# Six of eight layer norms turned by VectorE blocks and a trip through DRAM instead of by TensorE

## The chip, the core and the metric

The kernel runs on one core of a Trainium2 chip. The metric is the time of one execution on the device, in microseconds (us). The engines are named as the profile names them: PE is TensorE (PEld its weight loads), DVE is VectorE, ACT is ScalarE, POOL is GpSimd and SP is SyncE, whose queue issues most of the DMAs. Each engine works through its own list of instructions in order; an instruction that has to wait holds up all that stand behind it on the same engine.

## The reference: what is computed

For four sequences (b = 0 to 3) of 512 rows of 512 numbers, in float32, one block of a transformer with cross-attention:

```python
h1 = layer_norm(x, ln1_w, ln1_b)                    # over the 512 numbers of a row
q = h1 @ q_w + q_b;  k = enc @ k_w + k_b;  v = enc @ v_w + v_b   # 16 heads of 32
a = softmax(mask(q k^T / sqrt(32))) v
hidden = a @ cproj_w + cproj_b + x
y = layer_norm(hidden, ln2_w, ln2_b)
out = hidden + gelu(y @ fc_w + fc_b) @ proj_w + proj_b   # fc: 512 -> 2048, proj: 2048 -> 512
```

There are thus two layer norms per sequence, eight in all. They are called (1,b) and (2,b) here.

## The kernel before, in words

**What a turn is.** A matrix product on PE sums over the partitions, so the normalised rows (`xn`, rows on the partitions) have to be turned: features onto the partitions, rows along them. The four tiles of a norm (128 rows by 512 features, `t` = 0 to 3) become one tile of four feature groups (`d` = 0 to 3), each 128 by 512. For the first norms the target is `xT`, the second half of the tile `xe`; for the second norms it is `yT`. `ln_turn` (lines 150 to 161) does it for one `d`: four PE transposes into a PSUM tile `tp` (L156), then one eviction that also applies the norm's weight and bias, which after the turn belong to partitions: by DVE (L159) for d = 1 and 2, or by ACT (L161). For the norms in `BY_ACT`, (1,1) and (1,2), ACT does all four.

**The attention loop.** 16 head groups (`w` = 4b + g, four heads each) with four quarters of queries (`qt`) make 64 stages. A stage, called (w,qt), computes four score tiles on PE into the one PSUM tile `sc` (`scores`, L259); DVE adds the mask and finds the row minimum (L263, four times, called "minima"); ACT takes the exponential with its sum (L267, four times); DVE transposes the result in blocks of 32 by 32 (`turn`, L282 and L290) into `tb`. There are six slots for score tiles, and `sc` is single, so the next scores wait for the minima of the stage before. After two stages SP copies `tb` into `pT` with 16 DMAs, which swap the 32-partition blocks (L325), and some stages later PE multiplies with v (`attend`, L342) and DVE normalises (L347).

**What is laid between the stages.** For each head group `prep_k`, `prep_q`, `prep_v` (acck L215, accq L225, accv L237, some 3.5 us of PE each, evicted by ACT; POOL then adds the bias of v, L249). `prep_q` reads `xT`, so it needs the turned first norm of its sequence. After the four groups of a sequence comes `cproj` (accc L383, four chains), whose sum is `hidden`, then the second norm; then the chains `fc` (accf L449, reads `yT`) and `proj` (accp L459), taken a few at a time by `some(n)`. The order is written out by hand: `first[w]` is a list of work for head group w. A tuple gives one list for each of its four stages, run right after the stage's scores and block transposes were issued; a plain list is spread over the stages by cost, and `later[w]` is added to it from the third stage. `inputs(b)` returns the loads of x, the three parts of the first norm, its turn, and the load of enc.

**The end.** From about 558 us `last_mlps` computes the remaining MLP (half of sequence 1, and all of 2 and 3) by a scheme with seven products of blocks. `fc_pair` (L553) makes the hidden layer; `project` (L593) multiplies with proj in the order q1, q2, q3, q6, q7, q5, q4. Between q1 and q2 `sums` loads the next sequence's hidden rows, to which POOL adds a bias (L354); between q2 and q3 `turns` turns the second norm of the next sequence; POOL and DVE add the products to the hidden rows (`join`, L531), SP stores them; `middle` then makes the sums of blocks of `yT` (`y_sums`, DVE L481) and of the first weights (`sum_wa`, DVE L481 and L484), which the next `fc_pair` reads.

The statistics of a norm are DVE's (L125, L126), the reciprocal root is POOL's (L131, L133), and the normalisation DVE's (L147) or, for `BY_ACT`, ACT's (L143).

Of the kernel before, what the change touches and what calls it, by code (L numbers as in the profile page):

```python
# [12 lines left out]
F32 = mybir.dt.float32  # L13
U8 = mybir.dt.uint8
AF = mybir.ActivationFunctionType
# [5 lines left out]
P = 128  # L21
B, L, D, H = 4, 512, 512, 16
HD = D // H
INNER = 4 * D
NT = L // P
ND = D // P
# [5 lines left out]
NI = P // HD  # L32
# [15 lines left out]
LN1W, LN1B, QB, KB, LN2W, LN2B, FCB = 0, 4, 8, 12, 16, 20, 24  # L48
# [4 lines left out]
def xattn_block(ctx: ExitStack, tc: tile.TileContext, x, encT, mask, q_w, k_w, v_w, c_w, fc_w, p_w, vecs, rows, out):  # L53
    nc = tc.nc
    scale = float(np.float32(1.0) / np.sqrt(HD).astype(np.float32))

    def pools(stack, **bufs):
        return [stack.enter_context(tc.tile_pool(name=n, bufs=k)) for n, k in bufs.items()]

    const, keep, hids, tiles, small = pools(ctx, const=1, keep=1, hids=6, tiles=4, small=4)  # L60
    dram = ctx.enter_context(tc.tile_pool(name="dram", bufs=1, space=bass.MemoryType.DRAM))
    ps_acc = ctx.enter_context(tc.tile_pool(name="ps_acc", bufs=4, space=PSUM))

# [6 lines left out]
    vec = const.tile([P, NVEC], F32, tag="vec", name="vec")  # L70
# [9 lines left out]
    eT, xT = (xe[:, i * ND * L : (i + 1) * ND * L].rearrange("p (d l) -> p d l", d=ND) for i in range(2))  # L80
# [9 lines left out]
    def k_q(w, i):  # L90
        n = w % 4 * 2 + i
        return pbt[:, n * D : (n + 1) * D]
# [16 lines left out]
    def kqv_w(w, i):  # L109
        n = 4 * i + 2 + w % 2  # L110
        return ptt[:, n * D : (n + 1) * D].rearrange("p (d f) -> p d f", d=ND)

    S = {}
    count = [0, 0, 0]
# [12 lines left out]

    def ln_rs(key):

        ve = small.tile([P, NT], F32, tag="ve", name=f"ve{key[0]}_{key[1]}")  # L130
        nc.gpsimd.tensor_scalar(ve, S["mv", key][:, :, 1], EPS, 1.0, ALU.add, ALU.mult)  # L131
        rs = small.tile([P, NT], F32, tag="rs", name=f"rs{key[0]}_{key[1]}")
        nc.gpsimd.tensor_tensor(rs, ve, nhalf, ALU.pow)  # L133
        S["rs", key] = rs
        if key in BY_ACT:
            nm = small.tile([P, NT], F32, tag="nm", name=f"nm{key[0]}_{key[1]}")
            nc.gpsimd.tensor_tensor(nm, S["mv", key][:, :, 0], rs, ALU.mult)
            nc.gpsimd.tensor_scalar(nm, nm, -1.0, 0.0, ALU.mult, ALU.add)
            S["nm", key] = nm

    def ln_norm(key, t, dst, src):
        if key in BY_ACT:
            nc.scalar.activation(  # L143
                dst, src, AF.Identity, bias=S["nm", key][:, t : t + 1], scale=S["rs", key][:, t : t + 1]
            )
            return
        nc.vector.tensor_scalar(  # L147
            dst, src, S["mv", key][:, t, 0:1], S["rs", key][:, t : t + 1], ALU.subtract, ALU.mult
        )

    def ln_turn(key, d, xn, dst):

        w, bi = (LN1W, LN1B) if key[0] == 1 else (LN2W, LN2B)
        tp = acc_tile(f"tp{key[0]}_{key[1]}_{d}")
        for t in range(NT):
            nc.tensor.transpose(tp[:, ts(t, P)], xn[t][:, ts(d, P)], ident)  # L156
        wd, bd = vec[:, w + d : w + d + 1], vec[:, bi + d : bi + d + 1]
        if d in (1, 2) and key not in BY_ACT:
            nc.vector.tensor_scalar(dst[:, d, :], tp, wd, bd, ALU.mult, ALU.add)  # L159
        else:  # L160
            nc.scalar.activation(dst[:, d, :], tp, AF.Identity, bias=bd, scale=wd)  # L161


    def queue(b):
        return Q[0] if b else nc.sync

    def load_enc(b):
        for d in range(ND):
            queue(b).dma_start(out=eT[:, d, :], in_=encT[b, ts(d, P), :])

    def load_x(b):
        S["xn", b] = [tiles.tile([P, D], F32, tag="xn", name=f"xn1_{b}_{t}") for t in range(NT)]
        for t in range(NT):
            queue(b).dma_start(out=S["xn", b][t], in_=x[b, ts(t, P), :])

# [11 lines left out]
    def ln1_turn(b, d):  # L187
        ln_turn((1, b), d, S["xn", b], xT)
# [167 lines left out]
    def stays(b, t):  # L356

        return b == 0 or b == SPLIT and t < 2

    def load_h(b, *ts_):  # L360

        if ("xa", b) not in S:
            S["xa", b] = dram.tile([L, D], F32, tag=f"xa{b}", name=f"xa{b}")
        for t in ts_:
            if b == B - 1:

                S["h", b, t] = k_q(t // 2, t % 2)
            else:
                pool, tag = (hids, "hid") if stays(b, t) else (tiles, "xn")
                S["h", b, t] = pool.tile([P, D], F32, tag=tag, name=f"h_{b}_{t}")  # L370
# [17 lines left out]
    def load_xn(b):  # L388

        for t in range(NT):  # L390
            S["h", b, t] = tiles.tile([P, D], F32, tag="xn", name=f"hn_{b}_{t}")
            Q[0].dma_start(out=S["h", b, t], in_=S["xa", b][ts(t, P), :])

    def load_hid(b, ts_):
# [10 lines left out]

    def norm2(b, t):
        h = S["h", b, t]
        y = tiles.tile([P, D], F32, tag="xn", name=f"xn2_{b}_{t}") if stays(b, t) else h
        S.setdefault(("yn", b), {})[t] = y
        ln_norm((2, b), t, y, h)  # L410

    def proj_bias(b):
        for t in range(NT):
            if stays(b, t):
                add_row(S["hid", b, t], 1)

    def ln2_turn(b, d):
        if d == 0:
            S["yT", b] = keep.tile([P, ND, L], F32, tag="yT", name=f"yT_{b}")
        ln_turn((2, b), d, S["yn", b], S["yT", b])  # L420


    weights, products = [], []
# [281 lines left out]

    def C(b):
        return [(CHAIN, lambda t=t: cproj(b, t)) for t in range(NT)]

    def turns1(b):
        return [(TURN, lambda d=d: ln1_turn(b, d)) for d in range(ND)]  # L710

    def turns2(b):
        return [(TURN, lambda d=d: ln2_turn(b, d)) for d in range(ND)]

    def FC(b, q):
        return [(CHAIN, lambda f=f: fc(b, f)) for f in range(q * FQ, (q + 1) * FQ)]
# [3 lines left out]

    def inputs(b):
        ln = [(0.0, lambda part=part: ln1(b, part)) for part in range(3)]
        return do(lambda: load_x(b)), ln, turns1(b), do(lambda: load_enc(b))

    def run(work, budget=None):

# [33 lines left out]
    x1, x2, x3, x4 = inputs(1)  # L760
# [9 lines left out]
    first = [[] for _ in range(NW)]  # L770
    later = [[] for _ in range(NW)]
# [17 lines left out]
    def some(n):  # L789
        taken, mlp[:n] = mlp[:n], []  # L790
        return taken
# [24 lines left out]
    k, q, v = A(7)  # L816
    c, t2 = C(0), turns2(0)
    first[4] = x1 + [k, q, v] + x4
    later[4] = c[:1] + x2[:1] + c[1:2] + x2[1:2] + c[2:3] + x2[2:] + c[3:]
    k, q, v = A(8)  # L820
    first[5] = (
        [k] + stat(0, 0, 1, 2, 3) + rs(0) + x3 + norm(0, 0, 1, 2, 3) + [v], [q] + t2, some(2) + pb_(0), some(2)
    )
    k, q, v = A(9)
    x1, x2, x3, x4 = inputs(3)
    first[6] = [k, q] + some(4) + [v] + x1
    k, q, v = A(10)
    first[7] = [k, q] + x2[:1] + some(2) + x2[1:2] + some(3) + [v]

    k, q, v = A(11)  # L830
    first[8] = h_(1, 0, 1) + x2[2:] + [k, q] + x3[:2] + some(1) + x3[2:3] + [v] + x3[3:] + h_(1, 2, 3) + x4
    later[8] = cb(1) + C(1)
    k, q, v = A(12)
    first[9] = [q] + some(2) + [k] + some(2) + [v]
    k, q, v = A(13)
    first[10] = [k, q] + some(4) + [v]
    k, q, v = A(14)
    t2 = turns2(1)
    first[11] = (
        [k, q] + stat(1, 0, 1, 2, 3) + rs(1), some(2) + norm(1, 0, 1, 2, 3), some(1) + t2[:2] + [v],  # L840
        t2[2:] + pb_(1) + some(1) + h_(2, 2, 3, 0, 1)
    )

    k, q, v = A(15)
    c = C(2)
# [49 lines left out]
    c = C(B - 1)  # L895
# [49 lines left out]
```

## Time and profile before

| what | value |
|---|---|
| time, median of 3 runs | 810.9 us (808.69 to 811.1) |
| the profiled execution: time / span of its instructions | 810.09 us / 808.3 us |
| mean granted TensorE clock | 0.996 |
| busy: PE | 791.9 us (98% of the span) |
| busy: DVE, ACT, POOL | 553.6, 360.8, 98.0 us |
| PE transposes of the turns (L156) | 128, 18.7 us busy in all |
| DMA | 137.13 MB, mean 170 GB/s |
| POOL's own DMA queue (q0) | 2.82 MB |

The span runs from the first to the last instruction; the time of the execution is 1.79 us longer. A time such as "at 168 us" counts from the start of the span. Idle time of an engine is put down to what released it. A matmul's row gives the time from its start to its modelled end; the step from one row's start to the next is the time it takes from PE.

### The profile page before, as it was taken

How to read it: one execution, taken by the hardware profiler on the slowest of the kernel's cores; microseconds unless marked ns; L12 is line 12 of the kernel's file. 1: busy time of each engine (PE TensorE's matmuls, PEld its weight loads, DVE VectorE, ACT ScalarE, POOL GpSimd, SP SyncE). 2: the span in 40 equal slices, each digit the busy share in tenths (PEclk: the TensorE clock that was granted, in tenths of full speed). 3: DMA queues.
4: the chain of work that ended last, by engine and by line, in shares of the span. 5: the costliest groups of instructions: out<-in, count | busy, mean ns of one | idle time of the engine just before them, and what ended most of it. 6: DMA issues, size and time to landing. Idle time of an engine off the chain costs nothing.

```text
span 808.3 us, 11790 instructions
## 1 busy us (share of the span) xinstructions
PE 791.9 (98%) x4082; PEld 481.2 (60%) x4082; DVE 553.6 (68%) x1145; ACT 360.8 (45%) x785; POOL 98.0 (12%) x112
## 2 busy tenths in 40 slices
PE   9999999979999999999999999999999999999998
PEld 6545455544454544535554333446888888888887
DVE  3788998876678665877778997636738993368511
ACT  2666755638673646556643469600312330023200
POOL 1110030030000030001131000120050021200011
PEclk9999999989999999999999999999999999999999
DMA  9889989837797877778768799883335330023001
GB/s 329 287 222 244 241 219 265 225 96 185 185 245 176 223 201 191 176 197 201 177 140 218 196 259 226 216 252 117 108 100 181 107 117 14 27 79 92 1 14 39
DMA packets 60955, 137.13 MB, mean 170 GB/s; under 512 B 12464, under 2 KB 15664, under 8 KB 60768
## 3 DMA queue, kind: packets, MB, share of 16 engines
q1 hardware_dynamic: 59472, 132.43, 61.2%
q0 software_dynamic: 896, 2.82, 1.1%
q10 hardware_dynamic: 528, 1.14, 0.7%
q8 instruction: 32, 0.52, 0.3%
q14 instruction: 27, 0.22, 0.1%
HBM read 58.22 MB, written 6.82 MB: 80 GB/s over the span
## 4 chain that ended last, share of the span: by engine, by line
PE 80%; DVE 7%; SPq 7%; DMA 3%; issue 1%; POOL 0%; ACT 0%; DVEq 0%; POOLq 0%
PE q L553 15%; PE accf L449 9%; PE accp L459 8%; PE accc L383 7%; SPq L325 7%; PE av L342 6%; PE sc L259 6%; PE acck L215 4%; PE accq L225 4%; PE accv L237 4%; DVE ptt L263 3%; PE q5p L593 2%; PE q3p L593 2%; PE q7p L593 2%; PE q6p L593 2%; PE q1p L593 2%
## 5 line engine op out<-in xcount | busy, mean ns | idle before, releaser
L267 ACT ACTIVATE ptt<-ptt,mn 128x512 f32<-128x512 f32 x256 | 182.2, 713 | 142.8 <-DVE mn L263 142.6
L263 DVE CUSTOM_DVE_ANT_0 ptt<-sc,mb 128x512 f32<-128x512 f32 x256 | 161.1, 685 | 45.6 <-PE sc L259 45.5
L282 DVE STREAM_TRANSPOSE tb<-ptt 128x1024 f32<-128x1024 f32 x96 | 119.1, 1242 | 10.4 <-ACT ptt L267 8.0
L449 PE MATMUL accf<-yT,pbt 128*128 128x512 f32 x192 | 87.3, 601 | 0.0
L459 PE MATMUL accp<-pbt,gt 128*128 128x512 f32 x192 | 86.5, 600 | 0.0
L259 PE MATMUL sc<-pbt 32*128 32x512 f32 x512 | 73.1, 640 | 4.8 <-DVE mn L263 2.6
L553 PE MATMUL q<-ys,gt 128*128 128x256 f32 x320 | 75.1, 379 | 0.0
L553 PEld LDWEIGHTS q<-ys,gt 128*128 128x128 f32 x320 | 60.8, 190 | 8.3
L449 PEld LDWEIGHTS accf<-yT,pbt 128*128 128x128 f32 x192 | 35.0, 190 | 50.2 <-issue 45.4
L459 PEld LDWEIGHTS accp<-pbt,gt 128*128 128x128 f32 x192 | 35.2, 190 | 48.8 <-issue 45.8
L237 PEld LDWEIGHTS accv<-ptt,xe 128*128 128x128 f32 x512 | 58.9, 192 | 8.2 <-issue 5.4
L237 PE MATMUL accv<-ptt,xe 128*128 128x128 f32 x512 | 60.5, 276 | 0.0
L215 PE MATMUL acck<-xe,ptt 128*128 128x512 f32 x128 | 59.0, 603 | 0.0
L553 PE MATMUL q<-yT,gt 128*128 128x256 f32 x240 | 58.1, 379 | 0.5 <-DVE gt L481 0.5
L225 PE MATMUL accq<-xe,ptt 128*128 128x512 f32 x128 | 58.4, 599 | 0.0
L383 PE MATMUL accc<-wc,oT 128*128 128x512 f32 x128 | 56.6, 596 | 0.0
L249 POOL TENSOR_TENSOR v<-v,row 128x512 f32<-128x512 f32 x16 | 20.4, 1274 | 278.5 <-ACT v L242 278.4
L557 ACT ACTIVATE ga<-uc,vec 128x256 f32<-128x256 f32 x40 | 20.4, 511 | 75.5 <-DVE uc L531 75.5
L553 PEld LDWEIGHTS q<-yT,gt 128*128 128x128 f32 x240 | 45.5, 190 | 7.4 <-DVE gt L481 0.9
L342 PE MATMUL av<-pT,v 128*32 128x256 f32 x768 | 48.1, 392 | 1.6 <-DMA pT<-tb 1.5
L267 ACT ACTIVATION_READ_ACCUMULATOR ptt<-ptt,mn 128x1 f32 x256 | 48.3, 189 | 0.0
L564 ACT COPY p<-q 128x256 f32<-128x256 f32 x20 | 7.1, 354 | 92.0 <-PE q L553 92.0
(121 smaller groups left out, 957.9 us busy)
## 6 DMA issues: line engine op xcount, KB each, us to landing
pT<-tb SPq DMA_DIRECT2D x384, 136.0 KB, 2.4
pbt<-p_w_dram SPq DMA_DIRECT2D x40, 256.0 KB, 3.1
gt<-fc_w_dram SPq DMA_DIRECT2D x40, 256.0 KB, 2.7
gt<-tb SPq DMA_DIRECT2D x64, 136.0 KB, 3.4
xe<-tb SPq DMA_DIRECT2D x56, 136.0 KB, 3.3
pbt<-fc_w_dram SPq DMA_DIRECT2D x24, 256.0 KB, 4.3
ptt<-k_w_dram SPq DMA_DIRECT2D x16, 256.0 KB, 3.9
xe<-encT_dram SPq DMA_DIRECT2D x16, 256.0 KB, 4.8
```

The costliest lines, as they stand in the source:

```text
L215: nc.tensor.matmul(acc, S["wk", w][:, d, :], eT[:, d, :], start=(d == 0), stop=(d == ND - 1))
L225: nc.tensor.matmul(acc, S["wq", w][:, d, :], xT[:, d, :], start=(d == 0), stop=(d == ND - 1))
L237: nc.tensor.matmul(acc[:, ts(t, P)], eT[:, d, ts(t, P)], S["wv", w][:, d, :], start=(d == 0), stop=(d == ND - 1),)
L259: nc.tensor.matmul(sc[:, h, :], qT[r, ts(qt, P)], kT[r, :], start=True, stop=True)
L263: nc.vector.tensor_tensor_reduce(out=s, in0=sc[:, h, :], in1=S["mb", w // NG], scale=1.0, scalar=FMAX, op0=ALU.add, op1=ALU.min, accum_out=mn,
L267: nc.scalar.activation(s, s, AF.Exp, bias=mn, scale=-1.0, accum_out=sums[:, qt, h : h + 1])
L282: nc.vector.transpose(*two_heads[k])
L342: nc.tensor.matmul(av[ts(h, HD), : 2 * P].rearrange(shape, **kw), v[:, t, ts(h, HD)], p[t][h], start=(t == 0), stop=(t == NT - 1),)
L383: nc.tensor.matmul(acc, S["oT", b][:, g, ts(t, P)], wc[:, g, :], start=(g == 0), stop=(g == NG - 1))
L449: nc.tensor.matmul(acc, S["fcw", b, f][:, d, :], S["yT", b][:, d, :], start=(d == 0), stop=(d == ND - 1))
L459: nc.tensor.matmul(acc, gT[q % 2][:, k, ts(t, P)], S["pw", b, q * FQ + k], start=(k == 0), stop=(k == FQ - 1))
L553: nc.tensor.matmul(o, a[:, k], y[:, k], start=(k == 0), stop=(k == 1))
```

## The change: what it does

Norms (1,0) and (1,1) are turned as before. The other six, (1,2), (1,3) and (2,0) to (2,3), are turned in three steps:

- `ln_flip`: DVE transposes 32 by 32 blocks of each of the four tiles (four instructions of 128x512), into the target tile itself, in an order that puts each block row together;
- `ln_swap`: POOL's queue writes that tile to DRAM (one DMA of 128 rows of 8 KB, 1 MB) and, when it has landed, reads it back into a new tile `raw` with four DMAs of 32 partitions (256 KB each), so that the 32-partition blocks change places;
- `ln_affine`: ACT applies weight and bias from `raw` to the target, four instructions of 128x512.

The pool `tiles` with its four slots becomes the one tile `xnt` with four parts, used in turn; `raw` takes 8 KB of each partition, and the area for the descriptors of POOL's DMAs is set to 8192. The order of the work around the turns changes: in `first[4]` to `first[11]` the steps have places of their own.

```diff
+    xnt = const.tile([P, NT * D], F32, tag="xnt", name="xnt")
+    raw = const.tile([P, NT * D], F32, tag="raw", name="raw")
...
+    def ln_flip(key, xn, dst):
+
+        tmp = dst.rearrange("p d l -> p (d l)").rearrange("p (j c t q) -> p t c j q", j=NI, c=ND, t=NT)
+        for t in range(NT):
+            nc.vector.transpose(tmp[:, t], xn[t])
+
+    def ln_swap(key, dst):
+
+        turned = dram.tile([NI, HD, NI, D], F32, tag="turned", name=f"turned{key[0]}_{key[1]}")
+        nc.gpsimd.dma_start(out=turned.rearrange("i a j n -> (i a) (j n)"), in_=dst.rearrange("p d l -> p (d l)"))
+        for j in range(NI):
+            nc.gpsimd.dma_start(
+                out=raw[ts(j, HD), :].rearrange("p (i n) -> p i n", i=NI), in_=turned[:, :, j, :].rearrange("i a n -> a i n")
+            )
+
+    def ln_affine(key, dst):
+
+        w, bi = (LN1W, LN1B) if key[0] == 1 else (LN2W, LN2B)
+        rv = raw.rearrange("p (i c t q) -> p c t i q", i=NI, c=ND, t=NT)
+        for d in range(ND):
+            nc.scalar.activation(
+                dst[:, d, :].rearrange("p (t i q) -> p t i q", t=NT, i=NI), rv[:, d], AF.Identity,
+                bias=vec[:, bi + d : bi + d + 1], scale=vec[:, w + d : w + d + 1],
+            )
...
-    def ln2_turn(b, d):
-        if d == 0:
+    def ln2_turn(b, step):
+        if step == 0:
             S["yT", b] = keep.tile([P, ND, L], F32, tag="yT", name=f"yT_{b}")
-        ln_turn((2, b), d, S["yn", b], S["yT", b])
+            ln_flip((2, b), S["yn", b], S["yT", b])
+        elif step == 1:
+            ln_swap((2, b), S["yT", b])
+        else:
+            ln_affine((2, b), S["yT", b])
...
     first[4] = x1 + [k, q, v] + x4
-    later[4] = c[:1] + x2[:1] + c[1:2] + x2[1:2] + c[2:3] + x2[2:] + c[3:]
-    k, q, v = A(8)
+    later[4] = c[:1] + x2[:1] + c[1:2] + x2[1:2] + c[2:3] + x2[2:]
     first[5] = (
-        [k] + stat(0, 0, 1, 2, 3) + rs(0) + x3 + norm(0, 0, 1, 2, 3) + [v], [q] + t2, some(2) + pb_(0), some(2)
+        x3[:1] + c[3:] + stat(0, 0, 1, 2) + [k8] + x3[1:2], stat(0, 3) + rs(0) + norm(0, 0, 1, 2, 3) + [v8] + x3[2:],
+        t2[:1] + [q8, v9] + t2[1:2], [k9, q9] + t2[2:] + pb_(0)
     )
...
-    first[6] = [k, q] + some(4) + [v] + x1
+    first[6] = some(7) + x1
...
-    first[8] = h_(1, 0, 1) + x2[2:] + [k, q] + x3[:2] + some(1) + x3[2:3] + [v] + x3[3:] + h_(1, 2, 3) + x4
-    later[8] = cb(1) + C(1)
+    first[8] = h_(1, 0, 1) + x2[2:] + [k, q] + x3[:1] + some(1) + x3[1:2] + [v] + h_(1, 2, 3) + x4
+    later[8] = cb(1) + C(1) + x3[2:]
...
-    first[9] = [q] + some(2) + [k] + some(2) + [v]
+    first[9] = [q] + some(3) + [k] + some(2) + [v]
...
-        [k, q] + stat(1, 0, 1, 2, 3) + rs(1), some(2) + norm(1, 0, 1, 2, 3), some(1) + t2[:2] + [v],
+        [k, q] + stat(1, 0, 1, 2, 3) + rs(1), some(2) + norm(1, 0, 1, 2, 3), t2[:1] + some(1) + [v] + t2[1:2],
         t2[2:] + pb_(1) + some(1) + h_(2, 2, 3, 0, 1)
...
-    nc = bacc.Bacc("TRN2", target_bir_lowering=False, num_devices=1)
+    nc = bacc.Bacc("TRN2", target_bir_lowering=False, num_devices=1, dynamic_dma_scratch_size=8192)
```

Here `x3` and `t2` are now the three steps flip, swap and affine of a first and of a second norm, `c` the four chains of `cproj`, and `k8`, `q8`, `v8` the preparations of head group 8. In `last_mlps`, `turns` still calls the three steps of the next sequence's second norm between q2 and q3.

More of the change, by code (lines that the diff above doesn't have):

```diff
@@ L58, in pools @@
         return [stack.enter_context(tc.tile_pool(name=n, bufs=k)) for n, k in bufs.items()]
-    const, keep, hids, tiles, small = pools(ctx, const=1, keep=1, hids=6, tiles=4, small=4)
+    const, keep, hids, small = pools(ctx, const=1, keep=1, hids=6, small=4)
     dram = ctx.enter_context(tc.tile_pool(name="dram", bufs=1, space=bass.MemoryType.DRAM))
@@ L111, in kqv_w, with xn_tile @@
         return ptt[:, n * D : (n + 1) * D].rearrange("p (d f) -> p d f", d=ND)
+    xnt = const.tile([P, NT * D], F32, tag="xnt", name="xnt")
+    raw = const.tile([P, NT * D], F32, tag="raw", name="raw")
+    def xn_tile():
+        n = count[3] % NT
+        count[3] += 1
+        return xnt[:, n * D : (n + 1) * D]
     S = {}
-    count = [0, 0, 0]
+    count = [0, 0, 0, 0]
     Q = [nc.sync]
@@ L171, in load_x @@
     def load_x(b):
-        S["xn", b] = [tiles.tile([P, D], F32, tag="xn", name=f"xn1_{b}_{t}") for t in range(NT)]
+        S["xn", b] = [xn_tile() for t in range(NT)]
         for t in range(NT):
@@ L368, in load_h @@
             else:
-                pool, tag = (hids, "hid") if stays(b, t) else (tiles, "xn")
-                S["h", b, t] = pool.tile([P, D], F32, tag=tag, name=f"h_{b}_{t}")
+                S["h", b, t] = hids.tile([P, D], F32, tag="hid", name=f"h_{b}_{t}") if stays(b, t) else xn_tile()
             Q[0].dma_start(out=S["h", b, t], in_=x[b, ts(t, P), :])
@@ L390, in load_xn @@
         for t in range(NT):
-            S["h", b, t] = tiles.tile([P, D], F32, tag="xn", name=f"hn_{b}_{t}")
+            S["h", b, t] = xn_tile()
             Q[0].dma_start(out=S["h", b, t], in_=S["xa", b][ts(t, P), :])
@@ L407, in norm2 @@
         h = S["h", b, t]
-        y = tiles.tile([P, D], F32, tag="xn", name=f"xn2_{b}_{t}") if stays(b, t) else h
+        y = xn_tile() if stays(b, t) else h
         S.setdefault(("yn", b), {})[t] = y
@@ L710, in turns1, with flips1 @@
         return [(TURN, lambda d=d: ln1_turn(b, d)) for d in range(ND)]
+    def flips1(b):
+        return [
+            (0.0, lambda: ln_flip((1, b), S["xn", b], xT)),
+            (0.0, lambda: ln_swap((1, b), xT)),
+            (0.0, lambda: ln_affine((1, b), xT)),
+        ]
     def turns2(b):
-        return [(TURN, lambda d=d: ln2_turn(b, d)) for d in range(ND)]
+        return [(0.0, lambda n=n: ln2_turn(b, n)) for n in range(3)]
     def FC(b, q):
@@ L722, in inputs @@
         ln = [(0.0, lambda part=part: ln1(b, part)) for part in range(3)]
-        return do(lambda: load_x(b)), ln, turns1(b), do(lambda: load_enc(b))
+        return do(lambda: load_x(b)), ln, turns1(b) if b < 2 else flips1(b), do(lambda: load_enc(b))
     def run(work, budget=None):
@@ L816, in xattn_block @@
     k, q, v = A(7)
+    k8, q8, v8 = A(8)
+    k9, q9, v9 = A(9)
     c, t2 = C(0), turns2(0)
     first[4] = x1 + [k, q, v] + x4
-    later[4] = c[:1] + x2[:1] + c[1:2] + x2[1:2] + c[2:3] + x2[2:] + c[3:]
-    k, q, v = A(8)
+    later[4] = c[:1] + x2[:1] + c[1:2] + x2[1:2] + c[2:3] + x2[2:]
     first[5] = (
-        [k] + stat(0, 0, 1, 2, 3) + rs(0) + x3 + norm(0, 0, 1, 2, 3) + [v], [q] + t2, some(2) + pb_(0), some(2)
+        x3[:1] + c[3:] + stat(0, 0, 1, 2) + [k8] + x3[1:2], stat(0, 3) + rs(0) + norm(0, 0, 1, 2, 3) + [v8] + x3[2:],
+        t2[:1] + [q8, v9] + t2[1:2], [k9, q9] + t2[2:] + pb_(0)
     )
-    k, q, v = A(9)
     x1, x2, x3, x4 = inputs(3)
-    first[6] = [k, q] + some(4) + [v] + x1
+    first[6] = some(7) + x1
     k, q, v = A(10)
```

## The prediction

> **What bounds the kernel.** I read the busy lines first, then PE's groups by shape, then PE in order of time, then the DMAs.
>
> ```profile
> PE   9999999979999999999999999999999999999998
> PE 791.9 (98%) x4082; PEld 481.2 (60%) x4082; DVE 553.6 (68%) x1145; ACT 360.8 (45%) x785; POOL 98.0 (12%) x112
> L156 PE MATMUL tp<-ident,xn 128*128 128x128 f32 x88 | 12.9, 284 | 4.2 <-ACT pbt L228 3.6 <-DVE xn L147 0.5
> ```
>
> PE is busy in every slice but one, and the 16 us left are mostly in the start: whatever leaves PE shortens the time, and whatever makes PE wait lengthens it by as much. The third line says that the turns hold PE's one long wait. It lies in the turn of (2,0):
>
> ```profile
> 168.01 0.49 PE L156 MATMUL tp<-ident,xn 128*128 128x128 f32 x3
> 169.05 1.20 PE L156 MATMUL tp<-ident,xn 128*128 128x128 f32 x9 [0.55 <-DVE xn L147]
> 173.89 1.11 PE L156 MATMUL tp<-ident,xn 128*128 128x128 f32 x4 [3.64 <-ACT pbt L228]
> 174.93 3.64 PE L342 MATMUL av<-pT,v 128*32 128x256 f32 x32
> ```
>
> The windows of the same stretch:
>
> ```profile
> 174.00:176.00 2.00, 2.00 (x16) 1.20 (x20) 1.66 (x3) 1.28 (x2) 0.00 (x0) 0.50 0.00 0
> 176.00:179.00 3.00, 3.00 (x31) 1.20 (x24) 0.36 (x1) 0.00 (x0) 0.00 (x0) 0.54 0.00 0
> ```
>
> Here the third number from the end is the granted clock: PE runs at half speed after that wait: the next L342 and L259 take 1.8 us more than elsewhere (3.57 against 1.87, 1.17 against 1.07). A wait of 4.2 us cost 6.0. Waits of 0.8 to 1.6 us elsewhere in the trace have no such tail.
>
> **What is removed.** The time from the first transpose of each turn to the next other work on PE: (1,2) 1.75 us (157.99 to 159.74); (2,0) 6.92 and the 1.8 behind it; (1,3) 0.53 + 0.50 + 0.44 + 0.49 = 1.96; (2,1) 0.87 + 0.93 = 1.80; (2,2) and (2,3) 1.96 each. Sum **18.1 us**. With nothing added the profiled 810.09 would become 792.0.
>
> **What is added beside PE.** 24 DVE transposes at 0.62 (half of L282's 1.24 for 1024) are 14.9 us; ten evictions L159 at 0.80 leave. ACT gets 24 instructions at 0.74 (L143 reads the same shape from SBUF) for ten or so L161 fewer. Both have room (68% and 45%), so the work is hidden by PE's; with that cover gone a norm would cost its 2.5 + 3.0 us. What can reach PE is the latency R from the issue of the write to the landing of the last read.
>
> ```profile
> xa<-h POOLq DMA_DIRECT2D x6, 256.0 KB, 3.3
> hid<-xa SPq DMA_DIRECT2D x6, 256.0 KB, 4.7
> wc<-c_w_dram SPq DMA_DIRECT2D x1, 1024.0 KB, 7.2
> ```
>
> No row shows 1 MB out and back through POOL. Low end: the fastest 256 KB write of POOL (2.9), three more issues (0.55 each, L386), one 256 KB read (3.2): 7.8. High end: 7.2 for 1 MB, 1.7 for issues, 6.2 (reads of x in the first 40 us): 15.1. I take the nearest rows. Write: 3.3 for 256 KB plus 768 KB at the 400 GB/s of the best slices, 5.2. Reads: at 658.47 four 256 KB reads are issued 0.45 us apart and the second has landed at 663.67, 5.2 after the first issue; the fourth, a little later, 6.2. **R = 11.5** in quiet stretches, 13 at (2,1), where the DMAs are 89% busy. The five DMAs of a norm cost POOL 2.8 us and its wait; before that POOL's queue was nearly empty but in `project`.
>
> The Trainium skill, "DMA: Bandwidth & Descriptors", section "Anatomy of one DMA — SWDGE (gpsimd) path", gives about 2.0 us plus bytes at 436 GB/s for such a DMA. By it 1 MB takes 4.4 us each way, R would be some 9.3 (an estimate from that page), and the sum below would come out at about -9: the rule speaks for the change, and the 3.3 us measured for 256 KB (2.6 by the rule) against it.
>
> **Where PE waits for R.** Stage by stage, in the order of the changed kernel, each step with its duration before.
>
> (a) Before the scores (5,0) one chain of `cproj` fewer stands on PE, so L342 there comes 3.56 us earlier, at 147.96. SP issues its 16 copies until about 147.3, and they land some 2.7 later: a wait of 2.0 us.
>
> (b) (1,2). From the start of the scores (5,0): minima and block transposes end at +6.1 (153.38 to 159.5 before), the four flips at +8.6. PE does accc, acck8, scores, accv8, L342, scores and wants accq8 at +15.8. ACT's first affine is done at 8.6 + R + 0.74. Wait R - 6.4 = 5.1, and half clock 1.8. Behind the affine on ACT stand the exponentials of (5,2), which have to wait for DVE anyway (minima at +22.4).
>
> (c) (2,0). DVE reaches its flips only after statistics, normalisation, minima and transposes: end at +29.9. POOL's write is issued behind the bias of v9, which ends at +30.0. ACT's affine is done at 30.0 + 11.5 + 0.74 = 42.3. PE started accq8 at +20.9 and wants the first accf 18.2 later, at 39.1. Wait 3.2, and 1.8 for the clock, as the wait before was not much longer.
>
> (d) (1,3). Flip and affine are some 25 us apart: R is hidden by accf, accv, cproj. No wait.
>
> (e) (2,1). No fc is near, but the affine stands on ACT before the exponentials of (12,0). The write is issued behind the bias of v14 at 399.6; the affine starts at 399.6 + R; then 3.0 of affine, 2.9 of exponentials, 1.25 and 2.5 on DVE (transposes, minima (12,1)) before `sc` is free: 409.1 + R. PE wants the scores (12,2) at 419. Wait R - 9.5 = 3.5 with R = 13, and 1.8.
>
> (f) (2,2). Here POOL's queue decides.
>
> ```profile
> 586.89 5.21 POOL L354 TENSOR_TENSOR hl<-hl,row 128x512 f32<-128x512 f32 x4 [45.94 <-DMA hl<-xa]
> 592.65 1.41 POOL L531 TENSOR_TENSOR h<-p1p,h 128x256 f32<-128x256 f32 x2 [0.55 <-ACT yT L161]
> 599.82 1.41 POOL L531 TENSOR_TENSOR h<-u2p,h 128x256 f32<-128x256 f32 x2 [5.76 <-DVE h L531]
> 602.88 2.78 POOL L531 TENSOR_TENSOR hid<-u3p,hid 128x256 f32<-128x256 f32 x4 [1.64 <-DVE u3p L531]
> ```
>
> The write waits behind the four bias sums, until 592.1; the joins wait until the write has landed (5.2) and the reads are issued (2.2): 599.5. Then 5.6 of joins, 0.4 for DVE's last join, 2.65 for `y_sums`, 1.55 for `sum_wa`: 609.7. PE, 1.96 earlier than before, wants it at 608.7 (611.17 - 0.47 - 1.96). The next loads of `xa` (1 MB, from 591.4) run beside the write: I add 0.8. Wait 1.8, against 0.47 before: 1.3 more.
>
> (g) (2,3). Products are twice as long here; q3 to q4 are 35 us of cover. No wait.
>
> (h) The six turns move 12.6 MB more beside the copies of pT, whose landing PE now and then waits for (1.5 us in all before). I take 0.9.
>
> **Sum.** 2.0 + 6.9 + 5.0 + 5.3 + 1.3 + 0.9 = 21.4 added, 18.1 removed: +3.3. From the profiled 810.09: **813.4 us**. The median is 0.8 above the profiled run; I leave the sum at 813.4.
>
> The Trainium skill, "TensorE: Matmul & The Clock Gate", Part 1, has the clock halve after an idle window of about 3.4 us. The 4.2 us row agrees; by the rule the waits of 3.2 us might escape it. That would take 1.8 from (c), and the sum would be +1.5. No run here shows where between 1.6 and 4.2 us the limit lies.
>
> **The rivals.**
>
> 1. Forecast: four waits take back what leaves PE; R 10.5 to 14. By the same formulas 806 to 820. For it: even the low end of R, 7.8, is over the 6.4 that (b) covers. Chance 0.45.
>
> 2. R is 9 or less: (a) 2, (b) 2.6 without the clock, (c) DVE-bound 3.1 and no clock, (e) to (f) 0.5, (h) 0.5: 8.7 added, 810.09 - 18.1 + 8.7 = **800.7**. For it: DMA slices at 160 to 180 us are nearly empty (0.16 at 169 to 174). Against it: the 3.3 and 4.7 above. It decides from R under 9.5. Chance 0.34.
>
> 3. The round trip meets the other traffic, R 14.5 at (1,2) and (2,0), 16 at (2,1): (a) 2, (b) 8.1 + 1.8, (c) 6.2 + 1.8, (e) 6.5 + 1.8, (f) 3 + 0.9, (h) 1: 33.1 added, **825**. For it: 1 MB took 7.2 us when others loaded. Against: that was the crowded start. Decides from R over 14. Chance 0.15.
>
> 4. The PE time does not fall, because the flips delay the minima and PE waits for `sc` instead: a flip adds 2.5 us in a stage whose minima end some 3 us or more before the next scores; only in (1,3), where flips wait for accq11 and minima follow, could it show. That gives 18.1 removed, 2.5 x 4 added on top of the forecast's: 823. Against it: DVE's 32% idle. Chance 0.06. That the transposes do not leave PE at all is excluded: the changed order has 32 of 128 left.
>
> **How the numbers follow.** A measurement tells 0.3%, 2.4 us, from no change, so "same" is 807.7 to 812.5. Case 1 lies partly below (0.05), within (0.11), above (0.29); case 2 is faster (0.32) or just within (0.02); cases 3 and 4 are slower (0.21). Faster 0.37, same 0.13, slower 0.50. Range: 799 (case 2 with R = 8.5) to 826 (case 3); the forecast's own is 806 to 820.
>
> **What would show it.** L156 at 32 instructions and PE busy about 14 us less. In the waits: PE accq for ACT xe some 5 us, PE accf for ACT yT some 3, PE sc for DVE mn some 3 near (12,2), and the clock near 0.5 after them. In the DMA view, POOL's write at 5 to 6 us and its reads at 4 to 6. If the write lands in under 4 us, or PE waits under 2 us at accq8, the forecast is wrong towards case 2; if the affines are late by over 8 us, towards case 3.

## The result and the profile after

The changed kernel takes **840.9 us** (median, 838.93 to 842.76) against 810.3 for the kernel before, measured beside it: ratio **1.038** (95% interval 1.0344 to 1.0417). The forecast was 813.4, its range ended at 826. The profiled execution of the changed kernel has a span of 836.8 us, 28.5 more than before.

The page of the changed kernel, first PE's busy line, then the slices of PE, of the granted clock and of the DMA engines:

```profile
PE 791.1 (95%) x3986; PEld 474.5 (57%) x3986; DVE 559.1 (67%) x1159; ACT 364.0 (44%) x793; POOL 113.9 (14%) x142
...
PE   9999899956999996999979999999998999999998
...
PEclk9999999969899998999989999999999999999999
DMA  8988999797497796768697698995255522232001
```

96 transposes have left PE, as they should have: the group of PE transposes, by shape, is now

```profile
L164 PE MATMUL tp<-ident,xnt 128*128 128x128 f32 x32 | 4.1, 276 | 0.0
```

against 18.7 us for 128. Yet PE is busy for 791.1 us, only 0.8 less than before. Matmuls overlap, so not all of these 14.6 us could come off; but the run without the trip, described below, has the same matmuls and is busy for 780.4 us. The 10.7 us between the two are matmuls that take longer at half clock (the mean granted clock is 0.980 here, 0.998 there). And PE is idle for 836.8 - 791.1 = 45.7 us, before 16.4. These 29.3 us are the whole loss. The waits of PE (total us, times, longest) say what it waited for:

```profile
PE av L375 <- DMA ptt<-k_w_dram: 8.4, 1, 8.4
PE av L375 <- DMA pT<-tb: 7.5, 3, 6.4
PE accf L485 <- ACT yT L192: 7.0, 1, 7.0
PE av L375 <- DMA xnt<-x_dram: 4.4, 1, 4.4
PE q L589 <- DVE gt L517: 2.7, 1, 2.7
```

L375 is the product of `attend` (L342 before). Of what DMAs bring it reads only the copies of `tb`, mostly in `pT`; where the view names a load of weights or of x, that load was issued by SP behind the copies and landed last. So three lines, some 20 us, are copies of `pT` that landed late. In order of time (start, duration, idle time before):

```profile
174.43 3.64 PE L375 MATMUL av<-pT,v 128*32 128x256 f32 x32 [8.39 <-DMA ptt<-k_w_dram]
...
181.96 5.40 PE L258 MATMUL accq<-xe,ptt 128*128 128x512 f32 x8 [2.10 <-ACT xe L192]
...
209.01 9.41 PE L485 MATMUL accf<-yT,pbt 128*128 128x512 f32 x16 [7.01 <-ACT yT L192]
...
321.28 3.64 PE L375 MATMUL av<-pT,v 128*32 128x256 f32 x32 [6.36 <-DMA pT<-tb]
...
430.52 3.64 PE L375 MATMUL av<-pT,v 128*32 128x256 f32 x32 [4.44 <-DMA xnt<-x_dram]
```

L375 takes 1.93 us at full clock and 3.64 here: each of these waits costs some 1.7 us more behind it. The windows of two of them (busy us of PE, PEld, DVE, ACT, POOL, then granted clock, DMA share, GB/s):

```profile
166.00:174.00 8.00, 0.03 (x1) 0.00 (x0) 7.89 (x20) 3.82 (x10) 2.59 (x5) 0.70 0.97 288
...
201.00:209.00 8.00, 1.00 (x8) 0.17 (x8) 2.96 (x9) 0.85 (x2) 4.40 (x4) 0.86 1.04 220
```

While PE stands still, the DMA engines are full (0.97 and 1.04). In the kernel before, the turn of (2,0) stood at this place, and the DMA share was 0.24 from 168 to 174 us and 0 from 174 to 179. The trip itself, by its DMA issues (KB each, median us to landing):

```profile
raw<-turned POOLq DMA_DIRECT2D x24, 256.0 KB, 6.3
...
turned<-yT POOLq DMA_DIRECT2D x4, 1024.0 KB, 5.4
turned<-xe POOLq DMA_DIRECT2D x2, 1024.0 KB, 5.7
```

From the issue of the write to the first affine R is 15.4 us for (1,2), 15.3 for (2,0), 14.9 for (2,1) and 15.3 for (2,2).

Comparing the starts of the scores with those of the kernel before gives the place of the loss: +4.1 us at (6,0), +13.5 at (6,1), +12.5 at (8,3), +20.7 at (9,0), +22.9 at (11,3), +28.3 at (12,0), +28.5 at the end. The trips of (1,2) and (2,0) lie before the first two, that of (1,3) before (9,0), that of (2,1) is under way before (12,0). The last two norms neither gain nor lose.

### The profile page after: what moved, and what is told of

Its sections match the earlier page's. It is cut to its first block, busy times and chain, and to the rows that moved or that the text cites. A ratio compares the mean times of both kernels' runs of the same rounds, so it can differ in the third digit from the quotient of the medians.

```text
span 836.8 us, 11660 instructions
## 1 busy us (share of the span) xinstructions
PE 791.1 (95%) x3986; PEld 474.5 (57%) x3986; DVE 559.1 (67%) x1159; ACT 364.0 (44%) x793; POOL 113.9 (14%) x142
## 3 DMA queue, kind: packets, MB, share of 16 engines
q0 software_dynamic: 3680, 15.40, 6.4%
## 4 chain that ended last, share of the span: by engine, by line
PE 71%; DMA 11%; SPq 7%; DVE 6%; issue 2%; ACT 1%; POOL 1%; DVEq 0%; ACTq 0%; POOLq 0%
PE q L589 14%; PE accf L485 9%; PE accp L495 8%; SPq L358 7%; PE av L375 6%; PE sc L292 6%; PE accv L270 5%; PE accq L258 4%; PE acck L248 4%; PE accc L415 4%; DMA pT<-tb 3%; DMA raw<-turned 3%; DVE ptt L296 3%; DMA xe<-encT_dram 2%; PE q4p L629 2%; PE q5p L629 2%
## 5 line engine op out<-in xcount | busy, mean ns | idle before, releaser
L485 PE MATMUL accf<-yT,pbt 128*128 128x512 f32 x192 | 89.4, 614 | 7.0 <-ACT yT L192 7.0
L292 PE MATMUL sc<-pbt 32*128 32x512 f32 x512 | 75.1, 657 | 4.7 <-DVE mn L296 2.5
L375 PE MATMUL av<-pT,v 128*32 128x256 f32 x768 | 51.5, 413 | 21.0 <-DMA ptt<-k_w_dram 8.4
L485 PEld LDWEIGHTS accf<-yT,pbt 128*128 128x128 f32 x192 | 36.0, 194 | 59.2 <-issue 45.7
L258 PE MATMUL accq<-xe,ptt 128*128 128x512 f32 x128 | 60.2, 614 | 2.1 <-ACT xe L192 2.1
L375 PEld LDWEIGHTS av<-pT,v 128*32 128x32 f32 x768 | 25.2, 117 | 49.4 <-issue 35.7
L589 PEld LDWEIGHTS q<-yT,gt 128*128 128x128 f32 x240 | 45.2, 190 | 12.1 <-DVE gt L517 3.1
```

Source lines behind the costliest of these rows:

```text
L258: nc.tensor.matmul(acc, S["wq", w][:, d, :], xT[:, d, :], start=(d == 0), stop=(d == ND - 1))
L292: nc.tensor.matmul(sc[:, h, :], qT[r, ts(qt, P)], kT[r, :], start=True, stop=True)
L375: nc.tensor.matmul(av[ts(h, HD), : 2 * P].rearrange(shape, **kw), v[:, t, ts(h, HD)], p[t][h], start=(t == 0), stop=(t == NT - 1),)
L485: nc.tensor.matmul(acc, S["fcw", b, f][:, d, :], S["yT", b][:, d, :], start=(d == 0), stop=(d == ND - 1))
L589: nc.tensor.matmul(o, a[:, k], y[:, k], start=(k == 0), stop=(k == 1))
```

## The experiments

Two theories stood at the start. **Theory L**: the loss is latency, PE and ACT wait for the affines, as the forecast had it, only longer. **Theory A**: the trip takes time of the 16 DMA engines that the copies of `pT` need. A third, **theory O**: moving the chain `c[3:]` of `cproj` behind an `attend` keeps the single tile `oT` busy, so DVE, and with it the release of `pT`, comes late.

### The order alone, the flips without the trip, the traffic without the wait, and the chain put back

The order of the changed kernel with all turns on PE (`c[3:]` put ahead of the first turn):

```diff
-        for t in range(NT):
-            nc.vector.transpose(tmp[:, t], xn[t])
+        for d in range(ND):
+            ln_turn(key, d, xn, dst)
...
-        turned = dram.tile(...)   # the five DMAs, and the affine's four instructions, are left out
+        pass
```

> The changed order of work, with all turns on TensorE at the places of the flips (no flip, no trip; the moved cproj chain stands just ahead of the turn of (1,2)). Theory 1 (the new order itself makes PE wait for late copies of pT at (5,1) and at (9,0)): two such waits stay, 822 to 830 us. Theory 2 (the order is harmless, the trip through DRAM makes all the waits): within 3 us of the kernel before, 808 to 813.

Measured: 823.6 us, ratio 1.0158 (1.0124 to 1.0193). That is in the range of its theory 1, but not for its reason: `attend` waits for copies only 1.7 us in all. PE waits instead 5.9 us in the turns and 4.1 us at two products behind evictions of ACT. The order by itself is no gain; it fits only steps that do not stand on PE.

Flips and affines without any DMA; the affine works in place:

```diff
-        turned = dram.tile(...)   # and the five DMAs
+        pass
...
-                dst[:, d, :].rearrange("p (t i q) -> p t i q", t=NT, i=NI), rv[:, d], AF.Identity,
+                dst[:, d, :], dst[:, d, :], AF.Identity,
```

> The changed kernel without its 30 DMAs: the flips stay, ACT applies weight and bias in place (the 32-partition blocks are not swapped, so that part of the computation is left out). It has the new order but neither the latency nor the traffic of the trip. Theory 1: the waits at (5,1) and (9,0) stay, those at accf (7.0 us and the slow clock behind it) and at (12,0) go, 815 to 822 us. Theory 2: all waits go, 792 to 797, the 18.1 us that the turns took from PE being gained.

Measured: **802.9 us**, ratio 0.9907 (0.9878 to 0.9936), between the two theories' ranges. Only one wait of PE is large:

```profile
170.19 3.56 PE L369 MATMUL av<-pT,v 128*32 128x256 f32 x32 [5.27 <-DMA pT<-tb]
```

This is the first finding: even without a trip, 18.1 us of removed turns give 7.7. The copies for this product are issued by SP from 157.1 to 168.0, and with the turns gone PE arrives before they have landed. The waits of `attend` (L369) come to 9.6 us in this trace against 2.3 in the kernel before, 7.3 more, and the clock behind the long one costs 1.6: 8.9 together. 18.1 - 8.9 = 9.2, and the two profiled executions differ by 8.6.

The same, with the five DMAs of each norm back, from `raw` to DRAM and from there to `raw`, so that no other engine waits for them. POOL itself still waits for its write before it issues the reads:

```diff
+        nc.gpsimd.tensor_copy(raw[:, :1], dst[:, ND - 1, L - 1 :])
+        nc.gpsimd.dma_start(out=turned.rearrange("i a j n -> (i a) (j n)"), in_=raw)
```

> As the kernel without DMAs, but the same five DMAs per norm are issued by POOL when the flips are done, from and to raw, and nobody waits for them (the swap of blocks is still left out). The distance to the kernel without DMAs is what their traffic costs the other copies, the distance to the changed kernel what their latency costs. If traffic delays the copies of pT (waits of 6.4 at (9,0) and 4.4 at (12,0) in the changed kernel, and the slow clock behind them): 12 us or more above the kernel without DMAs. If only the latency counts: within 3 us of it.

Measured: **829.2 us**, ratio 1.0211 (1.0184 to 1.0238). The traffic alone costs 26.3 us. PE's long waits of this run are for copies, but for the last one:

```profile
152.78 3.40 PE L375 MATMUL av<-pT,v 128*32 128x256 f32 x32 [4.75 <-DMA ptt<-q_w_dram]
...
178.08 3.64 PE L375 MATMUL av<-pT,v 128*32 128x256 f32 x32 [8.77 <-DMA ptt<-k_w_dram]
...
313.70 3.50 PE L375 MATMUL av<-pT,v 128*32 128x256 f32 x32 [7.22 <-DMA pT<-tb]
...
439.85 3.57 PE L375 MATMUL av<-pT,v 128*32 128x256 f32 x32 [4.48 <-DMA pT<-tb]
...
633.61 1.36 PE L589 MATMUL q<-yT,gt 128*128 128x256 f32 x4 [3.08 <-DVE gt L517]
```

The first of them lies ahead of the first trip (POOL issues that write at 169.3), so these 6.4 us, with their clock, are scatter of this execution and not the trip's; its executions spread from 825.8 to 832.7. The next three stand at three of the four places where the changed kernel lost, the third of them one `attend` later. The last wait has nothing to do with copies of `pT`: it is in the tail, at (2,2), where POOL's joins stand behind POOL's own wait of 6.7 us for the write. With the half clock behind it, it accounts for most of the 4.4 us by which this run falls further behind the run without a trip after the last scores. So some 22 of the 26.3 us are late copies.

The windows of one stage, from the scores (8,3) to the `attend` behind them, first of the run without a trip, where PE then waits 1.1 us, then of this one:

```profile
289.00:296.00 7.00, 7.00 (x20) 2.92 (x16) 5.91 (x13) 5.89 (x13) 0.56 (x1) 1.00 0.89 209
```

```profile
296.00:304.00 8.00, 8.00 (x25) 3.27 (x24) 6.07 (x14) 3.52 (x10) 2.23 (x2) 1.00 1.01 237
304.00:312.00 8.00, 2.47 (x6) 0.76 (x4) 2.08 (x4) 2.65 (x4) 1.14 (x2) 0.88 0.92 265
```

Without the trip the DMA engines are 0.89 busy and the copies come nearly in time; with it they are full, and PE then stands still for what they carry. SP's rows say the same: the 16 copies for this `attend` take 13.5 us to issue without the trip (from 281.27) and 19.1 with it (from 291.75). The queue view gives the price, first without the trip, then with it (packets, MB, share of 16 engines):

```profile
q0 software_dynamic: 896, 2.82, 1.0%
```

```profile
q0 software_dynamic: 3680, 15.40, 6.3%
```

POOL's queue (q0) took 6.3% of 830.5 us on all 16 engines against 1.0% of 799.7, 44 us for six norms, 7.4 each. The four norms that lie among copies come to 29.5, against some 22 lost.

The changed kernel with the chain put back where it was:

```diff
-    later[4] = c[:1] + x2[:1] + c[1:2] + x2[1:2] + c[2:3] + x2[2:]
+    later[4] = c[:1] + x2[:1] + c[1:2] + x2[1:2] + c[2:3] + x2[2:] + c[3:]
...
-        x3[:1] + c[3:] + stat(0, 0, 1, 2) + [k8] + x3[1:2], ...
+        x3[:1] + stat(0, 0, 1, 2) + [k8] + x3[1:2], ...
```

> The changed kernel with the fourth cproj chain of sequence 0 put back ahead of (5,0). Theory: there it stood behind the first attend of sequence 1, whose result goes to the single tile oT that this chain still reads; DVE waited 5.1 us for it, the one pT was freed 4.3 us later, and PE waited 8.4 us for the copies. Put back, that wait falls to under 3 us, but the trip of (1,2), 15.4 us long, then makes PE wait at accq8 instead (about 6 to 9): net 0 to 6 us better than the changed kernel. If the copies were late by the trip's traffic alone: no change within 2 us, and the wait for pT stays.

Measured: 840.6 us, ratio 1.037 (1.0348 to 1.0392), and L375 still waits 7.8 us there, where under 3 was expected. SP begins these copies 4.8 us sooner (153.50 instead of 158.25), but PE arrives sooner too. Theory O falls: the chain's place makes no difference to the time.

So of the 30.6 us lost, order and flips gave 7.7, the traffic took 26.3, and what is left, 840.9 - 829.2 = 11.8, goes with the waits for the affines. Both theories hold a part, but their shares depend on the order of subtraction. The changed kernel's own trace, beside that of the run without a trip, has 26.4 us more of idle PE: 13.4 at `attend` (23.0 against 9.6), 10.1 for affines, 2.2 for `gt` in the tail and 0.6 for a load of enc. Slower matmuls add 10.7. By that count A holds about half of the waits, by the runs some two thirds of the loss.

### Half the traffic, SP's order, one hop, and the tail alone

The write alone (no reads, nobody waits):

```diff
-        for j in range(NI):
-            nc.gpsimd.dma_start(...)   # the four reads
```

> Left out: the move between partition quarters, so the blocks of the six norms stay unswapped; of the trip only the write (1 MB per norm, POOL's queue, from the buffer raw) is kept and nobody waits for it. It halves the dose of the run with all five DMAs, which took 829.2 against 802.9 without any. Theory A (the trip's bytes take time of the 16 DMA engines, which are 0.9 to 1.0 busy around four of the six norms, so the copies of pT land late): q0's share above that of the run without a trip was 44 us of 16 engines for six norms, half of it for the writes, so about half of the 26 us stays: 816, between 812 and 820. Rival B (the reads alone do the harm, since each touches only 32 partitions): within 4 us of the run without a trip, 803 to 807. Rival C (any POOL DMA there disturbs the copies, whatever its size): 825 or more.

Measured: 810.8 us (807.0 to 818.8), ratio 1.0016 (0.999 to 1.0042): 7.9 us for 3.1% of 811.4 less 8.0, that is 17 us of engine time. Just less than A's half, more than B's nothing. The reads thus take 27 us of engine time and cost 18. But the 4.4 us in the tail belong to these 18, since PE waits only 0.5 us there with the write alone. The other 14 are 0.52 us per us of engine time, not far from the write's 0.46.

Each step of a plain list has a cost, an estimate of its time on PE, by which the list is spread over the stages (the expectation calls it the planner's cost); flip and swap have 0. The changed kernel with this cost given back to (1,3), so that enc is loaded behind the copies as before:

```diff
-            (0.0, lambda: ln_flip((1, b), S["xn", b], xT)),
-            (0.0, lambda: ln_swap((1, b), xT)),
+            (2 * TURN, lambda: ln_flip((1, b), S["xn", b], xT)),
+            (2 * TURN, lambda: ln_swap((1, b), xT)),
```

> The changed kernel, but with the flip and the swap of (1,3) given the planner's cost of the turns that they replace, so that the loads of enc stand on SP's queue where they stood before. Rival D (it is the order on SP's queue, the loads of enc ahead of the copies of pT, that costs the 8 us at the scores (9,0)): about 832 to 834, and the wait of L375 near 320 under 2 us. Theory A (the DMA engines are full there in any order): 837 to 845, the wait stays at 5 us or more or turns up at the next L375.

Measured: **834.2 us**, ratio 1.0294 (1.0263 to 1.0325), 6.8 us less. PE at the scores (9,0):

```profile
315.84 1.93 PE L375 MATMUL av<-pT,v 128*32 128x256 f32 x32 [1.31 <-DMA pT<-tb]
```

instead of 6.36 and half clock. Rival D is right about this place. It doesn't contradict A: the run without a trip has the loads of enc ahead of the copies as well (issued at 279, the copies from 281) and waits 1.1 there. Neither the order nor the trip made the wait alone; both in front of the same copies did.

The trip replaced by direct copies, SBUF to SBUF, 1 MB in place of 2:

```diff
-        turned = dram.tile(...)   # and the five DMAs
+        for d in range(NI):
+            for i in range(NI):
+                j = (i + d) % NI
+                nc.gpsimd.dma_start(out=raw[ts(j, HD), ts(i, D)], in_=dst.rearrange("p d l -> p (d l)")[ts(i, HD), ts(j, D)])
```

> The changed kernel with the trip replaced by 16 copies of 64 KB on POOL's queue, from the flipped blocks straight to their partitions of raw: no DRAM, 1 MB per norm in place of 2 MB, one hop in place of two, but 16 issues in place of 5. Theory A: half the bytes give back about half of the 26 us; latency is 16 issues of 0.55 us and some 3 us of landing, 11.5 to 12 against 15, which gives back some 4 of the 11.8 us of waits: 840.9 - 13 - 4 = 824, between 818 and 830. Rival C (the count of POOL's DMAs does the harm): as the changed kernel or slower, 838 to 860, since 16 issues hold POOL 9 us.

Measured: **823.9 us**, ratio 1.0193 (1.0166 to 1.0219), and rival C falls: 16 DMAs of POOL are better than 5 when they move half the bytes. The time is A's, its shares are not: it had 13 us for the traffic and 4 for the latency. In the trace the waits for affines fall by 7.2 us, those of `attend` by 4.3 (23.0 to 18.7), and matmuls take 3.7 less. q0 takes 4.1% of 820.4 us, 26 us above the run without a trip, in place of 44; from the first issue to the affine it takes 12.1, 11.2 and 13.2 us at (1,2), (2,0) and (2,1), against 15.

The kernel before, with the trip for (2,2) and (2,3) only:

```diff
     def turns2(b):
+        if b >= 2:
+            return [(0.0, lambda n=n: ln2_trip(b, n)) for n in range(3)]
```

> The kernel before, with its order, and the flips, trip and affine for the norms (2,2) and (2,3) alone, where the DMA share is 0.5 or less. Theory A: no pT copies are left to delay; 3.9 us of PE leave, of which about 1 comes back in the wait behind POOL's queue: 810.3 - 3 = 807.3, ratio 0.995 to 0.998. Rival E (a trip costs some 4 us each also in a quiet stretch): 814 or more.

Measured: 810.5 us, ratio 1.0005 (0.9992 to 1.0017): neither 807 nor 814. No copies of `pT` are left here; what shows is the trip's latency. PE in order of time:

```profile
611.46 1.38 PE L589 MATMUL q<-yT,gt 128*128 128x256 f32 x4 [2.69 <-DVE gt L517]
612.63 5.10 PE L589 MATMUL q<-ys,gt 128*128 128x256 f32 x16
```

The same 16 matmuls take 3.62 us in the kernel before. A wait longer by 2.2 us and a clock that costs 1.7 take back the 3.9 removed. POOL's write stood behind its four bias sums until 591.46, and the affine began 13.6 us later, at 605.08.

### Wider reads, another queue, both remedies, and a version that wins

The four reads by columns into 128 partitions each, not by 32 partitions:

```diff
-                out=raw[ts(j, HD), :].rearrange("p (i n) -> p i n", i=NI), in_=turned[:, :, j, :].rearrange("i a n -> a i n")
+            nc.gpsimd.dma_start(out=raw[:, i * D : (i + 1) * D], in_=turned[i].rearrange("a j n -> j a n"))
```

> The changed kernel, but each of the four reads takes one quarter of the columns into all 128 partitions (before: all columns into one quarter of the partitions); the same bytes and the same five DMAs. So far 1 MB of writes alone cost 8 us and the reads the other 18 of the 26, while q0's time was 17 us for the writes and 27 for the reads. Theory A (time of the DMA engines): only as far as q0's time falls; with q0 unchanged 838 to 844, with the reads as cheap as the writes (q0 down by 10 us) 834 to 838. Rival B (reads into 32 partitions are the harm): 826 to 832, with R at 12 or less.

Measured: 849.8 us, ratio 1.0477 (1.0457 to 1.0497): slower by 9, which neither theory expected. q0's time did not grow (5.9% of 845.0 is 50 us, before 54), so engine time does not explain it; the landing does: the 24 reads take 8.1 us in the median from issue to landing, 6.3 before. R went to 16.7 and 17.7 us at (1,2) and (2,0), and PE's waits for the affines grew: accf 9.4 (7.0), accq 3.8 (2.1), q 2.6 (1.0). The waits of `attend` did not (22.7 after 23.0). The packets of one read rose from 80 to 272 (q0's 3680 and 8288, less 1760 of the run with the write alone, by 24). This adds to theory L's part of the loss.

The write alone on ACT's queue instead of POOL's:

```diff
-        nc.gpsimd.dma_start(out=turned.rearrange("i a j n -> (i a) (j n)"), in_=raw)
+        nc.scalar.dma_start(out=S["turned"].rearrange("i a j n -> (i a) (j n)"), in_=raw)
```

> The run with the write alone (blocks left unswapped, no reads), but the write issued on ACT's hardware queue just ahead of the affine instead of on POOL's software queue. Theory A (the bytes' time on the engines decides, not the queue): 808 to 814, as on POOL's queue. Rival C (a transfer of the software queue is what disturbs the copies): 803 to 806, as without a trip.

Measured: 814.3 us, ratio 1.0044 (1.003 to 1.0057), as on POOL's queue (1.0016), if not worse. It is not the software queue that disturbs the copies, though the two runs differ in time as well: ACT issues the writes of (1,2) and (1,3) some 5 and 16 us later than POOL did. The Trainium skill, "DMA: Bandwidth & Descriptors", section "Issuing engines are not separate DMA queues", says that transfers started by SP, ACT or POOL run on the same 16 engines and interleave; these two runs agree.

Direct copies together with that cost (in (2,2) and (2,3) ACT issues half of the copies):

```diff
-                nc.gpsimd.dma_start(out=raw[ts(j, HD), ts(i, D)], ...)
+                q = nc.gpsimd if i % 2 or key[0] == 1 or key[1] < 2 else nc.scalar
+                q.dma_start(out=raw[ts(j, HD), ts(i, D)], ...)
...
-            (0.0, lambda: ln_flip((1, b), S["xn", b], xT)),
+            (2 * TURN, lambda: ln_flip((1, b), S["xn", b], xT)),
```

> The changed kernel with direct copies (1 MB, one hop) and the planner's cost for flip and swap of (1,3) as well; in (2,2) and (2,3) half of the copies are issued by ACT. If what the two gave singly (17.1 and 6.8 us) adds up: 817, and some 2 less for (2,2): 813 to 819. If both only ease the same full engines: 820 to 825.

Measured: 818.1 us, ratio 1.0081 (1.0058 to 1.0103). The remedies add up, and the whole design still loses.

The kernel before with direct copies for (2,2) and (2,3) alone, half of them issued by ACT:

```diff
+                q = nc.gpsimd if i % 2 else nc.scalar
+                q.dma_start(out=raw[ts(j, HD), ts(i, D)], in_=dst.rearrange("p d l -> p (d l)")[ts(i, HD), ts(j, D)])
```

> The kernel before with (2,2) and (2,3) alone turned by flips and direct copies, 8 issued by POOL and 8 by ACT, which is idle there from 586 to 605. In the run with the trip for these two the affine of (2,2) started at 605.1 and PE waited 2.7 us at L589 and then ran 1.7 us slower at half clock, which took back the 3.9 us removed. Theory: ACT's copies follow the flips (590.1) by 5 us, POOL's the bias sums (591.5) by 4.5, all land by 599, the affine ends at 602 to 603 and PE waits for nothing: 810.4 - 3.9 = 806.5, ratio 0.994 to 0.997. Rival: the landing is later than the trip's, 604 or more, and nothing is gained: 809 to 812.

Measured: **805.8 us** (804.46 to 806.78), ratio **0.9941** (0.9926 to 0.9955), faster than both kernels, and 0.6% faster than the one before. ACT's queue, then PE:

```profile
590.36 5.03 ACTq L178 DMA_DIRECT2D raw<-yT  x8
599.28 2.93 ACT L185 ACTIVATE yT<-raw,vec 128x512 f32<-128x512 f32 x4 [12.69 <-DMA out_dram<-h]
```

```profile
608.88 1.13 PE L588 MATMUL q<-yT,gt 128*128 128x256 f32 x4 [0.47 <-DVE gt L516]
```

The affine begins 5.8 us earlier than with the trip, and PE is left with the 0.47 that it had waited before.

## Why the prediction was wrong, by its own steps

**The step that failed is (h)**: "The six turns move 12.6 MB more beside the copies of pT ... I take 0.9." It is 26.3 us between the run with the traffic and the one without, some 22 of them late copies; in the changed kernel itself `attend` waits 13.4 us more than without the trip, before the clock. The changed kernel got 6.8 us back when only the order on SP's queue was repaired. I priced the traffic by what PE had waited before (1.5 us; 2.3 with the wait that the view puts down to a load of weights), and not by what the DMA engines had left. The slices showed it: between 120 and 450 us they are 0.6 to 0.9 busy but for one, and shorter stretches are full (0.97 from 130 to 150 us). The empty stretch at 160 to 180 us, which rival 2 had for it, was empty because PE stood in the turn of (2,0) and the attention loop behind it made no copies (SP issued none from 165.5 to 179.1). That gap left with the turn.

**What is removed (18.1).** The transposes and their wait did leave. But PE's next event at that place was not costed: with the turns gone it meets the copies of `pT`, 5.3 us and 1.6 of half clock at the second `attend` of the stage, in the run without any trip. Step (a) had this wait (2.0), at one `attend` too early and too small.

**R = 11.5.** The write was right: 5.2 forecast, 5.4 and 5.7 measured. The reads were not: 6.2 forecast, 8.5 to 9.9 from the first issue to the affine, 8.8 even at (2,2), where no copies of `pT` are left. I took them from reads of 256 KB of which two had landed after 5.2, and four together take longer than "a little".

**(b)** 5.1 forecast, 2.1 measured at accq8, since PE had already stood 8.4 for the copies. **(c)** 3.2 forecast, 7.0 measured: its formula with R = 15.3 instead of 11.5 gives 7.0. **(d)** No wait for the affine, right, but 6.4 for the copies behind trip and enc. **(e)** PE has no wait for `sc` near (12,2); L375 waits 4.4 for copies instead. Its sum has a slip besides: 409.1 + R against 419 leaves R - 9.9, 3.1 and not 3.5. **(f)** 1.3 forecast; 3.2 in the changed kernel, with the clock 3.9 in the run with the tail alone, and the two tail norms gain nothing. **(g)** Right: (2,3) has no wait.

**Rivals.** Number 3 (R over 14.5) named the right R, and its 825 is the forecast's sum with it. That it comes nearest is in part luck: of its waits only the one at accf came as it had them; at accq8 it was 2.1 instead of 8.1, near (12,2) none instead of 6.5, and waits for copies, which it priced at 1, stood there. Rivals 2 and 4 did not occur: R was 15, and the waits for `sc` on the minima are 2.5 us, before 2.6.

Open: the reads alone, without the write, were not run, nor was the trip's traffic with the order on SP's queue repaired; so the 18 us for the reads are a difference of two runs, and how much of the 26.3 is left with that order is not known. The traffic run holds POOL as well as the DMA engines. Of the trip only the write was tried on another queue, so what the reads cost by holding POOL, beyond the wait in the tail, is open.

## What to carry to other kernels

When work leaves the bounding engine for the DMA engines, add up the DMA time per stage, not over the span: a megabyte out and back took 7.4 us of all 16 engines here, and where the copies of the next stage were already filling them, the bound moved from PE to the copies. An idle stretch of a queue that lies next to a wait goes away with the wait, so it is no room for new traffic. The same change pays where the engines are half empty, if its latency is cut to what the work beside it covers: one hop instead of two, half of it issued by an engine that has nothing to do. Here that was worth 0.6%.

## What the runs showed of the hardware

The clock's limit is not one duration. Every wait of PE of 3.6 us or more was followed by half clock. Between 2.0 and 3.3 us it went both ways, as with the L371 of the run with the write on POOL's queue and that of the run with the write on ACT's (1.93 us is full speed):

```profile
409.17 3.59 PE L371 MATMUL av<-pT,v 128*32 128x256 f32 x32 [2.48 <-DMA pT<-tb]
```

```profile
302.40 1.93 PE L371 MATMUL av<-pT,v 128*32 128x256 f32 x32 [3.29 <-DMA pT<-tb]
```

The Trainium skill, "TensorE: Matmul & The Clock Gate", Part 1, has the clock halve after an idle window of about 3.4 us which runs freely. That it depends on where the wait lies agrees with the two rows; that 2.5 us can be enough does not follow from a whole idle window of 3.4.

The Trainium skill, "DMA: Bandwidth & Descriptors", section "Anatomy of one DMA — SWDGE (gpsimd) path", has a fit that comes to 4.4 us for 1 MB and 2.6 for 256 KB (estimates). The writes took 5.4 and 5.7 (medians) and the reads 6.3 from issue to landing, among the copies and in fours; in the run with the trip in the tail alone 4.7 and 5.4.

With 16 direct copies on POOL's queue POOL itself waited, after 8 to 12 issues, for earlier copies to land (12 waits, 8.8 us in all), which is part of why they did not reach the affine sooner.
